# Two moves at the seam of a spectral kernel: constants and first weights made a stage earlier, and two engines reading a set of sums side by side

## The chip, the cores and the metric

The kernel runs on one core of a Trainium2 chip. The metric is device time in microseconds (us) of one launch, all transfers between HBM and the core's memory (SBUF) included. Five engines share the work: PE (matrix multiplies into PSUM[...]), ACT and DVE (elementwise work; both can read PSUM), POOL (elementwise work in SBUF) and SP, which here only issues DMA transfers. Each engine runs its own instructions in order and waits on semaphores for the others.

## The reference

Two layers on an image batch x of shape (16, 16, 256, 256), float32. Layer 0 adds a 3x3 circular convolution, done through FFTs, of the group-normalised input. Layer 1 adds a Laplace-pole layer. Cut to what matters:

```python
x = x + conv(_gn(x), L0_conv_weight)
v = _gn(x)
alpha = fft2(v)
A  = 1 / (omega1[:, None, None, None] - pole1[None])
Bm = 1 / (omega2[:, None, None, None] - pole2[None])
S = einsum('ikpq,oikp,xikq->oxik', residue, A, Bm)
residue1 = einsum('biox,oxik->bkox', alpha, S)
x1 = ifft2(residue1).real
x2 = transient(alpha, A, Bm, residue, exp(pole1 * ty), exp(pole2 * tx))
out = x + x1 + x2
```

For each frequency (o, x), S is a 16 x 16 complex matrix that mixes the input channels into the output channels. It is a sum over the poles q of a factor that depends on o and a factor Bm that depends on x.

## The kernel before

The kernel has four stages, one after the other. Stage 1 (0 to about 590 us) is the convolution and the statistics for the norms; it also makes tables, among them cD, the part of S that depends on o, and leaves v in HBM (vD). Stage 2, the forward transform (about 590 to 1213 us), takes v to frequencies: 64 units, each one channel i and four images b0. Stage 3, the mixing (to about 1895 us), applies S. Stage 4 transforms back and adds the transient part.

**Forward stage.** For each unit, `fold` (L734 to L755) adds and subtracts mirrored halves of the image: DVE makes most of it, POOL the second part of vq (L750 and L751 called with POOL). `lines` (L758) multiplies on PE (L762, L770), and ACT scales the result into t (L778). `columns` (L785) multiplies again on PE (L790 for the projections psd, L805 for ps_x); ACT copies the odd half to q (L818), and DVE combines both into spec (L822 to L825). `first_slots` (L828) corrects single frequencies on DVE (L833) and POOL (L834). After the last four images of a channel, `project` multiplies psd by coefficients on DVE (L850) and POOL adds to proj (L851), and spec is written to HBM (aD, L891, 4 MB). The loop works one unit ahead: in iteration u it folds unit u + 1, runs lines of unit u and columns of unit u - 1. PSUM: three banks for ps_y, four for ps_x, one for psd.

**Mixing stage.** The 256 x-frequencies are taken as 128 partitions of work in 32 groups g, each with four quarters n. For each group, `weights(g)` makes Bm times a mask: DVE computes the complex reciprocals in four steps (L957 to L973) and a last multiply spreads them over the mask, on POOL (L983); for group 0 three ACT copies (L979) and one POOL operation (L980) do this. For group 32, the frequency 128, POOL does it. `sums(n, w)` multiplies the weights with ct, the SBUF copy of cD (L1012): 16 small products into two PSUM banks, called odd = 0 and 1. `spread` (L1023) takes each bank into sg, the mixing matrices: ACT writes one half with a sign (L1027), DVE a partition-shuffled half (L1028). Both read the same bank, so they are ordered one after the other.

`first_sums` (L1030) prepares group 0. Frequencies 0 and 128 share a slot there, so it runs eight sets of sums (four with w, four with w128); for each bank it calls spread twice, for the main part (128 frequencies) and for two single columns (`other`). Between sets it runs the steps of weights(1). It also clears `pair` (abd for quarters 0 and 1, L1035) and abd2, abd3 (L1055) on POOL, loads group 0 of aD (L1076, L1081), and sums proj into accs (L1038). Then the loop over g and n runs, all in the order written (a manual schedule): sums for group g + 1; two spreads; four `mix` products (L1094) into four PSUM banks, each copied to yt by ACT or DVE (L1207); loads of group g + 1 (`load`, L1068) and the store of yt to HBM (`store`, L1106, four DMAs). yt has two buffers. All these DMAs are issued on SP, in the order of the code:

```python
if n == 1 and g < 31:
    load(g + 1, n)
store(g, n, yt)
if n > 1 and g < 31:
    load(g + 1, n)
```

`pair` serves quarters 0 and 1, so load(g + 1, 1) waits for quarter 1's products. Beside this, `make_exps` (L1135) makes tables of exponentials for stage 4, mostly on POOL, with ACT's table loads (L1172, L1175).

Each stage has its memory pools on a stack; stage 3's are opened after stage 2's have been closed, and a tile that comes to lie on memory of stage 2 waits for the last use there. Within stage 2 and 3 each engine keeps the written order, apart from the seam, where instructions of stage 3 may stand ahead of the last ones of stage 2.

Of the kernel before, what the change touches and what calls it, by code (L numbers as in the profile page):

```python
# [9 lines left out]
FP = mybir.dt.float32  # L10
# [6 lines left out]
B = 16  # L17
C = 16
# [6 lines left out]
def conv_then_laplace_kernel(ctx: ExitStack, tc: tile.TileContext, a: dict, out: bass.AP):  # L25
# [829 lines left out]
    units = [(i, b0) for i in range(C) for b0 in range(0, B, 4)]  # L855

    loaded = {u: load_v(*units[u], nc.sync if u else nc.gpsimd) for u in range(3)}
    vq = fold(*units[0], loaded.pop(0))
    nc.vector.memset(sgn[:, 0:1], -1.0)
    nc.vector.memset(sgn[:, 1:2], 1.0)  # L860
    rest = v_stats(B - 4, B, lambda: pa.tile([P, 512], FP, name="ps_y", tag="ps_y"))
    last = None
    for u in range(len(units) + 1):
        at = units[u] if u < len(units) else None
        if at is not None:
            now = vq
            t = lp.tile([P, 2, 4, 3, P], FP, name="t", tag="t")
            if u + 1 < len(units):
                vq = fold(*units[u + 1], loaded.pop(u + 1))
# [12 lines left out]
        if at is not None:  # L882
            for j in range(2, 4):
                lines(*at, now, t, j)
                if u < 2:
                    next(rest, None)
        if last is not None:
            first_slots(b0, spec, *done)
            if b0 == B - 4:
                project(i, psd)  # L890
                (nc.sync if i + 1 < C else nc.scalar).dma_start(  # L891
                    out=aD[:, 2 * i : 2 * i + 2].rearrange("p r n -> p (r n)"),
                    in_=spec.rearrange("p r f b -> p (r f b)"),
                )
        last = (*at, t) if at is not None else None
    p1.close()
    ptab.close()


    p2 = ExitStack()  # L900

    yp = pool(p2, "yt", 2)
    g0 = pool(p2, "sg0")
    a0 = pool(p2, "abd0")
    wp = pool(p2, "w", 2)
    ep = pool(p2, "exps")
    kp = pool(p2, "m_const")
    up = pool(p2, "uv")
    a1 = pool(p2, "abd2")
    zp = pool(p2, "between")  # L910
    tp = pool(p2, "ct")
    a2 = pool(p2, "abd3")
    g1 = pool(p2, "sg1")
    pg = pool(p2, "p_s", 4, space=PSUM)
    pm = pool(p2, "p_mix", 4, space=PSUM)

    def new_sg(g):
        return (g0, g1)[g % 2].tile([P, N, 2 * C], FP, name="sg", tag="sg")

    pair = a0.tile([P, 4, 4, 2, 16, B], FP, name="abd01", tag="abd01")
# [11 lines left out]
    omega(omg, omg, rd[:, 1:2])  # L934
# [8 lines left out]
    nc.vector.tensor_scalar(pims, p2k[:, :, 1], sset, None, ALU.mult)  # L943
    nc.vector.tensor_tensor(prU[:, 0], p2k[:, :, 0], p2k[:, :, 0], ALU.mult)

    nc.vector.tensor_scalar(prU[:, 1], p2k[:, :, 0], m0, -1.0, ALU.mult, ALU.mult)
    nc.vector.tensor_scalar(prU[:, 2], p2k[:, :, 0], m1, -1.0, ALU.mult, ALU.mult)

    def weights(g):

        shape = [P, 32, 4]
        u = up.tile([P, 4, 32, 4], FP, name="u", tag="u")
        w, den, e, f = (u[:, j] for j in range(4))
        pr2, pre, pim = (prU[:, j].unsqueeze(2).to_broadcast(shape) for j in range(3))
        nc.vector.tensor_tensor(  # L957
            w,
            omg[:, g].unsqueeze(1).to_broadcast(shape),
            pims.unsqueeze(2).to_broadcast(shape),  # L960
            ALU.subtract,
        )
        nc.vector.tensor_tensor(den, w, w, ALU.mult)
        nc.vector.tensor_tensor(den, den, pr2, ALU.add)
        yield
        nc.vector.reciprocal(den, den)

        nc.vector.scalar_tensor_tensor(e, w, m1, pre, ALU.mult, ALU.add)
        nc.vector.scalar_tensor_tensor(f, w, nm0, pim, ALU.mult, ALU.add)
        yield  # L970
        v = up.tile([P, 32, 2, 4], FP, name="v", tag="v")
        nc.vector.tensor_tensor(v[:, :, 0], e, den, ALU.mult)
        nc.vector.tensor_tensor(v[:, :, 1], f, den, ALU.mult)  # L973
        wt = wp.tile([P, 4, 8, 32], FP, name="w", tag="w")
        v2 = v.rearrange("p a r s -> p a (r s)")
        w4 = wt.rearrange("p a k (i m) -> p (a k) i m", i=4)
        if g == 0:
            for i in range(3):
                nc.scalar.activation(w4[:, :, i], v2, AF.Copy, scale=m4[:, i : i + 1])  # L979
            nc.gpsimd.tensor_scalar(w4[:, :, 3], v2, m4[:, 3:4], None, ALU.mult)  # L980
            return wt
        full = [P, 32, 4, 8]
        nc.gpsimd.tensor_tensor(  # L983
            w4,
            v2.unsqueeze(2).to_broadcast(full),
            m4.unsqueeze(1).unsqueeze(3).to_broadcast(full),
            ALU.mult,
        )
        return wt

    def next_step(steps, w):
# [31 lines left out]
    def spread(to, n, odd, src):  # L1023


        k = 4 * n + 2 * odd
        nc.scalar.activation(to[..., k : k + 2], src, AF.Copy, scale=nsgn)  # L1027
        nc.vector.stream_shuffle(to[..., C + k : C + k + 2], src, swap)  # L1028

    def first_sums():  # L1030
# [3 lines left out]
        wt, w128 = at_once(weights(0)), at_once(weights(32))  # L1034
        nc.gpsimd.memset(pair, 0.0)  # L1035
        load(0, 1)
# [4 lines left out]
        for h, w in enumerate((wt, w128)):  # L1041
            for n in range(4):
                fy = slice(P * h, P * h + P)
                ps = sums(n, w)
                for odd in range(2):
                    spread(sg[:, fy], n, odd, ps[odd][:, :, fy].rearrange("p q n -> p n q"))
                    spread(other[:, 1 - h], n, odd, ps[odd][:, :, P * (1 - h)])
# [20 lines left out]
    def load(g, jq):  # L1068
# [4 lines left out]
        for s in range(4):  # L1073
# [122 lines left out]
    for g in range(32):  # L1196
# [3 lines left out]
        for n in range(4):  # L1200
            evict = sums(n, w_now) if ahead is not None else []
            yt = yp.tile([P, 2, 4 * B, 16], FP, name="yt", tag="yt")
            for odd, ps in enumerate(evict):
                spread(ahead, n, odd, ps.rearrange("p q n -> p n q"))
# [3 lines left out]
            if n == 1 and g < 31:  # L1208
                load(g + 1, n)
            store(g, n, yt)  # L1210
            if n > 1 and g < 31:
                load(g + 1, n)
# [372 lines left out]
```

## Time and profile before

| what | us |
|---|---|
| median of 3 runs | 2682.2 (2677.55 to 2683.32) |
| the profiled execution | 2672.83 |
| its span, first to last instruction | 2670.8 |
| PE busy | 2492.1 (93%) |
| DVE busy | 1991.5 (75%) |
| ACT busy | 1448.6 (54%) |
| POOL busy | 1310.0 (49%) |
| last forward matmul (L805) starts | 1211.57, for 1.95 |
| first matmul of sums (L1012) starts | 1224.58 |
| first mixing matmul (L1094) starts | 1252.27 |

The profile gives, for one execution, when each instruction ran and what it waited for. "POOL L851 TENSOR_TENSOR proj<-proj,pr ... x2 [0.99 <-DVE pr L850]" reads: POOL ran two additions of line 851 that write proj; before them it sat idle 0.99 us, until DVE's pr of line 850 was there. SPq, ACTq are the DMA-issuing queues of SP and ACT. A chain of 60% PE means that most of the chain of work that ended last is PE's.

### The profile page before, as it was taken

What the parts mean: (1) busy time and instruction counts of PE and PEld (TensorE: products, weight loads), DVE (VectorE), ACT (ScalarE), POOL (GpSimd) and SP (SyncE); (2) the same over time, 40 slices, a digit from 0 to 9 for tenths busy, and PEclk for the clock granted to TensorE, in tenths of its full rate; (3) what the DMA queues carried; (4) which work ended last, traced back from release to release, by engine and by line L of the source; (5) the groups of instructions that cost most, each with busy time, mean ns of one, the idle gap of its engine ahead of it and who ended that gap; (6) DMA issues with size and microseconds to landing.
All of it is one profiled execution on the core that took longest, in us unless ns stands there. A gap on an engine that the chain in (4) does not pass through costs nothing.

```text
span 2670.8 us, 84449 instructions
## 1 busy us (share of the span) xinstructions
PE 2492.1 (93%) x35314; PEld 1877.6 (70%) x35314; DVE 1991.5 (75%) x3805; ACT 1448.6 (54%) x2726; POOL 1310.0 (49%) x1182
## 2 busy tenths in 40 slices
PE   5998899889999999997999999999699999999998
PEld 2444454457777777774877778887588888888887
DVE  7767689748888888887788778787366776666666
ACT  2565566566666666664666656666244444444443
POOL 1333368342333333333566755766546565555653
PEclk9999999989999999997999999999899999999999
DMA  7888978865556655664777777777889999898985
GB/s 273 276 278 275 282 251 301 270 207 174 212 198 237 237 207 196 245 229 154 216 230 224 226 223 232 213 223 228 233 279 287 288 287 290 278 291 283 293 279 178
DMA packets 476828, 653.17 MB, mean 245 GB/s; under 512 B 51063, under 2 KB 426999, under 8 KB 466593
## 3 DMA queue, kind: packets, MB, share of 16 engines
q1 hardware_dynamic: 475376, 640.58, 74.9%
q8 instruction: 278, 4.55, 0.7%
q0 software_dynamic: 928, 3.02, 0.4%
q10 hardware_dynamic: 144, 4.19, 0.4%
q14 instruction: 102, 0.83, 0.1%
HBM read 368.15 MB, written 280.36 MB: 243 GB/s over the span
## 4 chain that ended last, share of the span: by engine, by line
PE 60%; DMA 15%; DVE 13%; SPq 4%; issue 3%; POOL 3%; ACT 2%; DVEq 0%; ACTq 0%; POOLq 0%
PE ps_conv L294 14%; PE ps_y L762 9%; PE ps_mix L1094 8%; PE ps_y L770 8%; DMA yk<-yD 6%; PE ps_x L805 4%; DMA out_y<-ol 4%; DMA yD<-yt 4%; PE ps_p L1337 3%; DVE r L1370 3%; PE ps_f L1361 3%; PE ps_f L1362 3%; PE ps_s L1012 2%; DVE ol L1373 2%; DVE sg L1028 2%
## 5 line engine op out<-in xcount | busy, mean ns | idle before, releaser
L1094 PE MATMUL ps_mix<-abd,sg 128*64 128x128 f32 x8192 | 482.2, 276 | 35.5 <-ACT yt L1207 25.1
L1094 PEld LDWEIGHTS ps_mix<-abd,sg 128*64 128x64 f32 x8192 | 448.2, 138 | 92.7 <-ACT yt L1207 49.9
L1301 POOL TENSOR_TENSOR u<-yk 128x512 f32<-128x512 f32 (+1 forms) x268 | 346.3, 1323 | 311.6 <-PE ps_p L1337 203.9
L294 PE MATMUL ps_conv<-xt,wc 32*32 32x512 f32 x12288 | 449.1, 615 | 47.7 <-issue 41.6
L294 PEld LDWEIGHTS ps_conv<-xt,wc 32*32 32x32 f32 x12288 | 251.1, 104 | 234.0 <-issue 153.5
L778 ACT ACTIVATE t<-ps_y,vmr 128x384 f32<-128x384 f32 x512 | 297.5, 581 | 162.7 <-PE ps_y L770 162.6
L1028 DVE STREAM_SHUFFLE sg<-ps_s 128x512 f32<-128x512 f32 (+1 forms) x264 | 326.0, 1325 | 0.0
L762 PE MATMUL ps_y<-tabE,vq 128*128 128x256 f32 x1024 | 313.5, 388 | 13.2 <-DVE vq L751 11.7
L264 POOL TENSOR_TENSOR vt<-vt 128x1024 f32<-128x1024 f32 x64 | 151.7, 2371 | 324.8 <-DVE vsum L261 256.0
L770 PE MATMUL ps_y<-tabO,vq 128*128 128x256 f32 x1024 | 306.0, 381 | 0.0
L1337 PEld LDWEIGHTS ps_p<-inv,u 128*128 128x128 f32 x2048 | 266.2, 193 | 50.4 <-issue 25.5
L1361 PE MATMUL ps_f<-pt,inv 128*128 128x256 f32 x1008 | 301.3, 381 | 0.0
L1362 PE MATMUL ps_f<-hs,ey 128*128 128x256 f32 x1008 | 300.4, 380 | 0.0
L1365 DVE TENSOR_TENSOR r<-ps_f,q 128x256 f32<-128x256 f32 x256 | 107.3, 419 | 254.6 <-ACT q L1364 254.6
L1337 PE MATMUL ps_p<-inv,u 128*128 128x128 f32 x2048 | 279.5, 280 | 13.2 <-POOL u L1305 13.1
L1207 ACT COPY yt<-ps_mix 128x512 f32<-128x512 f32 x352 | 191.2, 593 | 152.0 <-DMA yD<-yt 100.5
L309 ACT ACTIVATE vt<-ps_conv,xq 128x512 f32<-128x512 f32 x256 | 162.2, 684 | 181.4 <-PE ps_conv L294 181.4
L1364 ACT COPY q<-ps_f 128x256 f32<-128x256 f32 x256 | 95.4, 373 | 290.6 <-PE ps_f L1362 284.7
L762 PEld LDWEIGHTS ps_y<-tabE,vq 128*128 128x128 f32 x1024 | 189.7, 191 | 89.7 <-ACT q L818 50.3
L750 POOL TENSOR_TENSOR vq<-vf 128x512 f32<-128x512 f32 x64 | 81.4, 1272 | 293.2 <-DVE vf L754 270.6
L1339 ACT COPY pt<-ps_p 128x512 f32<-128x512 f32 x256 | 150.2, 587 | 137.1 <-PE ps_p L1337 132.7
L770 PEld LDWEIGHTS ps_y<-tabO,vq 128*128 128x128 f32 x1024 | 195.6, 191 | 27.0
(239 smaller groups left out, 4067.5 us busy)
## 6 DMA issues: line engine op xcount, KB each, us to landing
yD<-yt SPq DMA_DIRECT2D x512, 128.0 KB, 3.4
vl<-vD SPq DMA_DIRECT2D x256, 256.0 KB, 3.8
out_y<-ol SPq DMA_DIRECT2D x128, 512.0 KB, 10.0
s<-vD SPq DMA_DIRECT2D x252, 256.0 KB, 5.9
aD<-spec SPq DMA_DIRECT2D x15, 4096.0 KB, 13.1
yk<-yD SPq DMA_DIRECT2D x60, 1024.0 KB, 8.4
xt<-in_x SPq DMA_DIRECT2D x64, 645.0 KB, 6.2
xt<-in_x SPq DMA_DIRECT2D x64, 516.0 KB, 6.9
```

The source lines that it names most:

```text
L294: nc.tensor.matmul(acc[r][32 * c : 32 * c + 32], lhsT=ready[b][0][rows, phase, tap], rhs=halves[b][u // 2][rows, q : q + 5 : 4, 2 - tap : ...
L309: nc.scalar.activation(vt[:, r % 2], acc[r], AF.Identity, bias=ready[b][1])
L762: nc.tensor.matmul(ps[:, 0:N], lhsT=vf[:, xo, 0, j], rhs=tabE[:, 0 : i + 2 : i + 1], start=True, stop=False, skip_group_check=True,)
L770: nc.tensor.matmul(ps[:, P : P + N], lhsT=vf[:, xo, 1, j], rhs=tabO[:, i : C + 1 : C - i], start=False, stop=True, skip_group_check=True,)
L778: nc.scalar.activation(t[:, xo, j].rearrange("p l n -> p (l n)"), ps[:, 0:384], AF.Copy, scale=vmr[:, 0, b0 + j, i : i + 1],)
L1028: nc.vector.stream_shuffle(to[..., C + k : C + k + 2], src, swap)
L1094: nc.tensor.matmul(ps[64 * t : 64 * t + 64, j], lhsT=sg[:, f : f + 2].rearrange("p f m -> p (f m)"), rhs=abd[jq][:, :, 2 * t + cc, 2 * jj ...
L1207: (nc.vector.tensor_copy if m >= (2 if late else 3) else nc.scalar.copy)(o, src)
L1301: nc.gpsimd.tensor_tensor(u[:, :, j].rearrange("p b (c n) -> p c b n", c=8), in0, in1, o)
L1337: nc.tensor.matmul(ps[:, at], lhsT=u[:, n], rhs=tab, start=True, stop=True)
L1361: nc.tensor.matmul(ps[:, e], lhsT=tab, rhs=pt[:, e], start=True, stop=False)
L1362: nc.tensor.matmul(ps[:, e], lhsT=ey[:, e], rhs=hs, start=False, stop=True)
```

## The change

1. The pools for the mixing's constants (`m_const`) and weights (`uv`) are opened before the forward loop, on the other side of the memory. The three constant loads, `weights` and the constant operations move with them. `first_constants` is called in iteration 60; the first three steps of weights(0) run in iterations 61, 62 and 63. The masks of group 0 are now four ACT copies, and POOL's one operation goes.
2. `spread` takes both banks of a set: ACT reads bank 0 while DVE reads bank 1, and then they swap.
3. The clearing of `pair` stands ahead of the weights in `first_sums`.
4. In the loop, load(g + 1, 1) is split: rows 0 and 1 ahead of the store of quarter 1, rows 2 and 3 behind it.

```diff
@@ before the forward loop @@
     units = [(i, b0) for i in range(C) for b0 in range(0, B, 4)]
+    p2 = ExitStack()
+    kp = pool(p2, "m_const", side="right")
+    up = pool(p2, "uv", side="right")
+
+    p2k = kp.tile([P, 32, 2], FP, name="p2k", tag="p2k")
+    nc.sync.dma_start(out=p2k, in_=a["pole2_k"])
+    omg = kp.tile([P, 33, 4], FP, name="kgrp", tag="kgrp")
+    nc.sync.dma_start(out=omg, in_=a["kgrp"])
+    mcol = kp.tile([P, 11], FP, name="mcol", tag="mcol")
+    nc.sync.dma_start(out=mcol, in_=a["mcol"])
...
+    def first_constants():
+        omega(omg, omg, rd[:, 1:2])
+        nc.vector.tensor_scalar(pims, p2k[:, :, 1], sset, None, ALU.mult)
+        nc.vector.tensor_tensor(prU[:, 0], p2k[:, :, 0], p2k[:, :, 0], ALU.mult)
+
+        nc.vector.tensor_scalar(prU[:, 1], p2k[:, :, 0], m0, -1.0, ALU.mult, ALU.mult)
+        nc.vector.tensor_scalar(prU[:, 2], p2k[:, :, 0], m1, -1.0, ALU.mult, ALU.mult)
+
+    def weights(g):
...
+        nc.vector.tensor_tensor(v[:, :, 0], e, den, ALU.mult)
+        nc.vector.tensor_tensor(v[:, :, 1], f, den, ALU.mult)
+        if g == 0:
+            yield
+        wt = wp.tile([P, 4, 8, 32], FP, name="w", tag="w")
...
+        if g == 0:
+            for i in range(4):
+                nc.scalar.activation(w4[:, :, i], v2, AF.Copy, scale=m4[:, i : i + 1])
+            return wt
...
-    last = None
+    last, first_weights = None, weights(0)
     for u in range(len(units) + 1):
...
+        if u == len(units) - 4:
+            first_constants()
+        if len(units) - 4 < u < len(units):
+            next(first_weights)
         if last is not None:
             first_slots(b0, spec, *done)
...
-    def spread(to, n, odd, src):
-
-
-        k = 4 * n + 2 * odd
-        nc.scalar.activation(to[..., k : k + 2], src, AF.Copy, scale=nsgn)
-        nc.vector.stream_shuffle(to[..., C + k : C + k + 2], src, swap)
+    def spread(n, *pairs):
+
+
+        for odd in range(2):
+            for to, src in pairs:
+                k = 4 * n + 2 * odd
+                nc.scalar.activation(to[..., k : k + 2], src[odd], AF.Copy, scale=nsgn)
+            for to, src in pairs:
+                k = 4 * n + 2 * (1 - odd)
+                nc.vector.stream_shuffle(to[..., C + k : C + k + 2], src[1 - odd], swap)
...
-        wt, w128 = at_once(weights(0)), at_once(weights(32))
         nc.gpsimd.memset(pair, 0.0)
+        wt, w128 = at_once(first_weights), at_once(weights(32))
         load(0, 1)
...
-                for odd in range(2):
-                    spread(sg[:, fy], n, odd, ps[odd][:, :, fy].rearrange("p q n -> p n q"))
-                    spread(other[:, 1 - h], n, odd, ps[odd][:, :, P * (1 - h)])
+                spread(
+                    n,
+                    (sg[:, fy], [z[:, :, fy].rearrange("p q n -> p n q") for z in ps]),
+                    (other[:, 1 - h], [z[:, :, P * (1 - h)] for z in ps]),
+                )
...
-    def load(g, jq):
+    def load(g, jq, rows=range(4)):
...
-        for s in range(4):
+        for s in rows:
...
-            for odd, ps in enumerate(evict):
-                spread(ahead, n, odd, ps.rearrange("p q n -> p n q"))
+            if evict:
+                spread(n, (ahead, [z.rearrange("p q n -> p n q") for z in evict]))
...
             if n == 1 and g < 31:
-                load(g + 1, n)
+                load(g + 1, n, (0, 1))
             store(g, n, yt)
-            if n > 1 and g < 31:
-                load(g + 1, n)
+            if g < 31:
+                load(g + 1, n, (2, 3) if n == 1 else range(4))
```

More of the change, by code (lines that the diff above doesn't have):

```diff
@@ L855, in conv_then_laplace_kernel @@
     units = [(i, b0) for i in range(C) for b0 in range(0, B, 4)]
+    p2 = ExitStack()
[7 more added lines that the diff above has]
+    nc.sync.dma_start(out=mcol, in_=a["mcol"])
+    m4, sset, fixrow = mcol[:, 0:4], mcol[:, 4:5], mcol[:, 5:6]
@@ new lines, in conv_then_laplace_kernel @@
+    nsgn, first = mcol[:, 7:8], mcol[:, 8:9]
+    osgn, nosgn = mcol[:, 9:10], mcol[:, 10:11]
+    m0, m1, nm0 = cols[:, 0:1], cols[:, 1:2], cols[:, 9:10]
+    prU = kp.tile([P, 4, 32], FP, name="prU", tag="prU")
+    pims = kp.tile([P, 32], FP, name="pims", tag="pims")
+    def first_constants():
[4 more added lines that the diff above has]
+        nc.vector.tensor_scalar(prU[:, 2], p2k[:, :, 0], m1, -1.0, ALU.mult, ALU.mult)
@@ new lines, in weights @@
+    def weights(g):
+        shape = [P, 32, 4]
+        u = up.tile([P, 4, 32, 4], FP, name="u", tag="u")
+        w, den, e, f = (u[:, j] for j in range(4))
+        pr2, pre, pim = (prU[:, j].unsqueeze(2).to_broadcast(shape) for j in range(3))
+        nc.vector.tensor_tensor(
+            w,
+            omg[:, g].unsqueeze(1).to_broadcast(shape),
+            pims.unsqueeze(2).to_broadcast(shape),
+            ALU.subtract,
+        )
+        nc.vector.tensor_tensor(den, w, w, ALU.mult)
+        nc.vector.tensor_tensor(den, den, pr2, ALU.add)
+        yield
+        nc.vector.reciprocal(den, den)
+        nc.vector.scalar_tensor_tensor(e, w, m1, pre, ALU.mult, ALU.add)
+        nc.vector.scalar_tensor_tensor(f, w, nm0, pim, ALU.mult, ALU.add)
+        yield
+        v = up.tile([P, 32, 2, 4], FP, name="v", tag="v")
+        nc.vector.tensor_tensor(v[:, :, 0], e, den, ALU.mult)
+        nc.vector.tensor_tensor(v[:, :, 1], f, den, ALU.mult)
+        if g == 0:
+            yield
+        wt = wp.tile([P, 4, 8, 32], FP, name="w", tag="w")
+        v2 = v.rearrange("p a r s -> p a (r s)")
+        w4 = wt.rearrange("p a k (i m) -> p (a k) i m", i=4)
+        if g == 0:
+            for i in range(4):
+                nc.scalar.activation(w4[:, :, i], v2, AF.Copy, scale=m4[:, i : i + 1])
+            return wt
+        full = [P, 32, 4, 8]
+        nc.gpsimd.tensor_tensor(
+            w4,
+            v2.unsqueeze(2).to_broadcast(full),
+            m4.unsqueeze(1).unsqueeze(3).to_broadcast(full),
+            ALU.mult,
+        )
+        return wt
@@ L897, in conv_then_laplace_kernel @@
     ptab.close()
-    p2 = ExitStack()
     yp = pool(p2, "yt", 2)
@@ L906, in conv_then_laplace_kernel @@
     ep = pool(p2, "exps")
-    kp = pool(p2, "m_const")
-    up = pool(p2, "uv")
     a1 = pool(p2, "abd2")
@@ L929, in conv_then_laplace_kernel @@
     nc.sync.dma_start(out=ct, in_=cD)
-    p2k = kp.tile([P, 32, 2], FP, name="p2k", tag="p2k")
-    nc.sync.dma_start(out=p2k, in_=a["pole2_k"])
-    omg = kp.tile([P, 33, 4], FP, name="kgrp", tag="kgrp")
-    nc.sync.dma_start(out=omg, in_=a["kgrp"])
-    omega(omg, omg, rd[:, 1:2])
-    mcol = kp.tile([P, 11], FP, name="mcol", tag="mcol")
-    nc.sync.dma_start(out=mcol, in_=a["mcol"])
-    m4, sset, fixrow = mcol[:, 0:4], mcol[:, 4:5], mcol[:, 5:6]
-    nsgn, first = mcol[:, 7:8], mcol[:, 8:9]
@@ L939, in conv_then_laplace_kernel @@
-    osgn, nosgn = mcol[:, 9:10], mcol[:, 10:11]
-    m0, m1, nm0 = cols[:, 0:1], cols[:, 1:2], cols[:, 9:10]
-    prU = kp.tile([P, 4, 32], FP, name="prU", tag="prU")
-    pims = kp.tile([P, 32], FP, name="pims", tag="pims")
[L943 to L989, printed above, removed]
@@ L1044, in first_sums @@
                 ps = sums(n, w)
-                for odd in range(2):
-                    spread(sg[:, fy], n, odd, ps[odd][:, :, fy].rearrange("p q n -> p n q"))
-                    spread(other[:, 1 - h], n, odd, ps[odd][:, :, P * (1 - h)])
+                spread(
+                    n,
+                    (sg[:, fy], [z[:, :, fy].rearrange("p q n -> p n q") for z in ps]),
+                    (other[:, 1 - h], [z[:, :, P * (1 - h)] for z in ps]),
+                )
                 if 4 * h + n in (3, 4, 5):
```

## The prediction

> **What bounds the kernel now.** I read busy time by stretch first, cut where the engines' timelines change their lines. Columns: stretch, its length, then busy time (and instructions) of PE, PE's weight loads, DVE, ACT, POOL; granted clock; DMA share; GB/s.
>
> ```profile
> 590.00:1211.60 621.60, 615.37 (x4088) 443.76 (x4088) 522.40 (x1191) 371.56 (x639) 220.16 (x282) 0.99 0.61 216
> 1211.60:1252.30 40.70, 24.26 (x316) 10.35 (x313) 30.15 (x109) 12.74 (x37) 18.80 (x10) 0.66 0.33 130
> 1252.30:1891.00 638.70, 602.18 (x12152) 508.51 (x12160) 497.00 (x904) 405.55 (x680) 384.35 (x295) 0.99 0.77 224
> ```
>
> The forward stage is PE's (99% busy). The mixing loop is nearly PE's: 36.5 us without a matmul in 638.7. Between them lies a seam of 40.7 us, where PE's few matmuls are stretched by waits. The change touches the seam and the loop.
>
> Second, the seam's timelines. DVE, with rows left out between:
>
> ```profile
> 1217.92 0.98 DVE L75 TENSOR_SCALAR kgrp<-kgrp,rd 128x132 f32<-128x132 f32 x1
> 1218.82 1.25 DVE L943 TENSOR_SCALAR pims<-p2k,mcol 128x32 f32<-128x32 f32 x1
> ...
> 1222.85 0.29 DVE L973 TENSOR_TENSOR v<-u 128x128 f32<-128x128 f32 x1
> ...
> 1227.14 0.75 DVE L1028 STREAM_SHUFFLE sg<-ps_s 128x256 f32<-128x256 f32 x1
> ...
> 1251.69 0.19 DVE L1052 TENSOR_TENSOR other<-other,sg 128x32 f32<-128x32 f32 x1
> ```
>
> POOL and ACT there:
>
> ```profile
> 1217.55 2.48 POOL L851 TENSOR_TENSOR proj<-proj,pr 128x512 f32<-128x512 f32 x2 [0.99 <-DVE pr L850]
> 1223.40 0.94 POOL L980 TENSOR_SCALAR w<-v,mcol 128x256 f32<-128x256 f32 x1 [3.37 <-DVE v L973]
> 1226.34 2.18 POOL L983 TENSOR_TENSOR w<-v,mcol 128x1024 f32<-128x1024 f32 x1 [2.00 <-DVE v L973]
> 1228.46 6.92 POOL L1035 MEMSET abd<- 128x8192 f32 x1
> ```
>
> ```profile
> 1216.89 0.34 ACTq L891 DMA_DIRECT2D aD<-spec  x1
> ...
> 1227.92 0.26 ACT L1027 ACTIVATE other<-ps_s,mcol 128x2 f32<-128x2 f32 x1 [0.82 <-DVE sg L1028]
> ```
>
> The reader is to see: PE's last forward matmul ends at 1213.5, yet its first sum starts at 1224.58, behind constants, weights and POOL's copy of them. Then ACT and DVE take turns: ACT waits for DVE 0.82 us, DVE for ACT. Eight sets of sums take 1227.14 to 1251.65.
>
> Third, the loop: its waits (who waited for whom: total us, times, longest), the SP queue, and one stall.
>
> ```profile
> ACT yt L1207 <- DMA yD<-yt: 100.5, 51, 8.5
> DVE sg L1028 <- ACT sg L1027: 90.0, 68, 3.7
> PE ps_mix L1094 <- ACT yt L1207: 25.1, 22, 5.8
> ```
>
> ```profile
> 1282.18 3.17 SPq L1076 DMA_DIRECT2D abd<-aD  x4
> 1285.46 5.41 SPq L1108 DMA_DIRECT2D yD<-yt  x8
> ```
>
> ```profile
> 1291.92 3.71 PE L1094 MATMUL ps_mix<-abd,sg 128*64 128x128 f32 x64 [1.84 <-ACT yt L1207]
> ```
>
> Four loads (3.2 us) stand in SP's queue before the stores of quarter n=1. Those land about 1291.2, so ACT can first write that yt buffer again, for n=3, at 1291.29. PE wants the bank, for the next group's n=0, and stalls 1.84. I counted PE's gaps over 0.15 us by place in the group: n=0 18.5 us in 19 gaps; n=1 6.2 in 7; n=3 4.1 in 8, and 5.8 at the loop's very end.
>
> **What the skill says.** The Trainium skill, "PSUM — Partial Sum Buffer", section "PSUM bank collisions raise a hardware error", says that two engines must not touch one bank and quadrant at once, ACT and DVE reads included. So turn-taking is kept within a bank; the trace agrees (the 0.82 us waits). "SBUF — State Buffer", section "SBUF: two separate sides": DVE and GpSimd share a port pair under an exclusive lock; a DVE op with two SBUF inputs is held only against a GpSimd op that reads SBUF. The trace fits: L75 and L943 took 0.98 and 1.25 us, each ending with one of POOL's proj additions, while L1052, with two SBUF inputs, took 0.19 during a memset.
>
> **The change part by part.**
>
> *Forward stage.* Five constant operations enter unit 60: 0.18 to 0.23 us each by the prU rows, starts 0.10 to 0.15 apart, so 0.8 us. They push the fold on DVE, then POOL's half (L750, L751), which ended 1190.94. PE needed it from about 1191.85, so 0.9 of slack covers them. First weights in unit 61 take 0.95 us (three operations); PE's slack at the next fold is 2.2, of which 1.8 is used. Unit 62's step falls into a 6.15 us DVE gap. I take +0.5, bounds 0 and +2 (a lock wait on top). The three constant DMAs move from behind ct to SP's queue before a pair of vD stores at about 524; their 1.2 us of issue fit a 3.6 us gap there: nothing.
>
> *Start of the seam.* In the order listing of the changed program, DVE makes v(0) and all of weights(32) before the last spec operations; ACT makes the four copies of w before the last q copies. DVE has 3.44 us idle there (1209.95 to 1213.38) and needs 0.4 + 2.9; ACT has 1.84 idle and needs 4 x 0.41 = 1.7. They just fit. PE's first sums can then start near 1213.5. But POOL's order becomes: memset (6.92), the last two corrections of spec, w(32), proj. The memset starts when POOL is free, 1209.8 to 1210.4, and ends about 1217.2. Corrections to 1217.6 (before 1216.57), w(32) 2.0 to 1219.6, proj 2.48 to 1222.1. accs (L1038 before) waits for proj, 0.7, and the shuffles queue behind accs: first shuffle 1222.8 instead of 1227.14. Gain 4.3.
>
> *Eight sets.* The same 32 main and small pairs, but in each half ACT reads one bank while DVE reads the other, then they swap. A half costs DVE about 0.7 (0.75 + 0.16 with the overlap of consecutive starts), so a set about 1.4; before, two turns of 1.43 made 2.9. 8 x 1.4 + 2.5 for the three steps of weights(1) = 13.7, and the row fixes 0.8: 1237.3. PE must still run its projection matmuls (3.5) and the loop's first sums (1.0) after the last set, which puts the first mixing matmul at about 1238.6 against 1252.3. The loads it needs: the last aD write, issued 0.7 later, lands 13.1 on, 1230.8; SP issues four loads in 2.5, last landing 4.3 on: 1237.6. This floor is a microsecond under. Seam: -13.7; bounds -10 (set costs 1.8) and -15 (the load floor). If the memset did hold DVE's weights, spec and aD would be 6.5 late and the seam would give only about 7.
>
> *The loop's load split.* Two of four loads go behind the stores of n=1: stores start up to 1.25 us earlier. Each n=0 gap shrinks by at most that: 18.5 becomes 2.5, so at most 16. The two later loads end about 9 us after n=1's mixing; they are needed 10.4 after. Because SP issues as many DMAs as before, and a removed stall exposes the next wait (POOL's w, ACT's table loads), I count 8.
>
> *The loop's evictions.* DVE no longer waits for ACT's first copy (90 us of waiting), but DVE idles later instead, for PE's fourth tile, so most of it is no gain; where ACT is late behind a table load, DVE's first shuffle is free, which should take part of the n=1 gaps: 3 us. Against this, ACT's second copy now waits for DVE's first shuffle (1.31 us against 0.57 spacing): yt copies behind it on ACT, and so the stores, start 0.7 later, more when DVE is held by a reciprocal. ACT is 63% busy there, and PE hides it while ACT's third copy ends within the 4.67 us of a quarter; 2.04 + 3 x 0.55 = 3.7 does. Cost 1, bounds 0 and 30. Loop: -10, bounds -22 (the n=0 and n=1 gaps gone) and +15.
>
> Sum: 0.5 - 13.7 - 10 = -23. The profiled execution took 2672.83 (span 2670.8), so 2649.8; the runs' median is 2682.2, 0.35% higher, so 2659 there.
>
> **Rivals.**
> 1. Only the seam gives; the loop is unchanged because SP's queue stays as full (28 issues of about 0.5 us in 18.7): 2682 - 13 = 2669. For it: stores in runs of eight with SP seldom idle. Against: the gaps sit at one place in the group.
> 2. POOL's early memset decides: spec, aD and proj late, the seam gives 5 to 7, the loop little: 2674. Against: L1052's 0.19.
> 3. More: all gaps at n=0 and n=1 go: 2682 - 36 = 2646. Against: SP.
> 4. Slower: ACT is held by DVE. It decides from the point where DVE reaches the first shuffle over 1 us after PE's sums are ready: then 1 + 1.31 + 0.7 + 1.65 fills a quarter. At 0.25 us in each of 124 sets it costs 31 us, against the seam's 13.7 and 2 from the load split: 2682 + 15 = 2697. For it: DVE is the busiest of the three (78%), and its 128x128 operations stretch from 0.28 to 1.3 us beside POOL's exponentials. Against: the wait list shows ACT late more often than DVE.
>
> **How the numbers follow.** Forecast 0.50, seam alone 0.21, memset 0.09, more 0.08, slower 0.12. About 0.2% (5 us) can be told from no change here. Forecast, seam and more are faster; of memset's 0.09 0.04 is faster, 0.05 the same; slower keeps 0.11 and gives 0.01 to no change: 0.83, 0.06, 0.11. The range runs from 2644 (rival 3 with the runs' spread of 3) to 2677 (memset, same spread).
>
> **What would show it.** Right: sums at about 1213.5, first shuffle near 1223, first mixing matmul 1237 to 1240; no turn of ACT and DVE on the small copies; n=0 gaps mostly gone. Wrong: forward PE gaps over 2 us at lines L762; new waits of ACT's sg copy on DVE's shuffle that end in PE gaps; abd loads arriving after PE asks; DVE's weights stretched beside the memset. A loop longer than 640 us would make the sign wrong.

## The result, and the profile after

The changed kernel took 2663.39 us (median of 15 runs, 2654.82 to 2673.96) against 2679.33 for the kernel before on the same chips (15 runs, 2672.73 to 2686.58). The ratio is 0.9946, with a 95% interval of 0.9932 to 0.9959: 14.5 us faster by the ratio, give or take 3.6. The forecast was 23 us faster.

The one profiled execution of each kernel must not be set against the other as a whole. The one before took 2672.83 and is near the fast end of its kind. The one after took 2673.96 and is the slowest of its 15. So the stages are compared, cut at the same events in each trace. The table has the execution before and the one after; the last column is the spread over the other profiled executions of this study.

| stretch, from event to event | before | after | how much it moves where the program has the same text |
|---|---|---|---|
| start to first ps_y (stage 1) | 594.3 | 598.2 | 587.2 to 600.5 |
| forward: to the start of the last L805 group | 617.2 | 617.6 | 617.0 to 618.0 |
| seam: to the first mixing matmul | 40.7 | 38.5 | within 0.25, one execution 1.5 off |
| mixing: to the end of the last one | 638.6 | 640.2 | 638.6 to 650.7 with the old loop |
| the rest | 780.0 | 777.4 | 769.8 to 777.8 |

The forward stage and the seam can be read from one trace to a fraction of a microsecond. Stage 1 and the last stage move by 8 to 13 us from one execution to the next, without any change to their instructions. What the change does to the mixing loop is therefore read from medians, after taking the seam out.

Busy time by stretch, of the kernel after, with the columns of the same view before (length; PE, weight loads, DVE, ACT, POOL; clock; DMA share; GB/s):

```profile
598.25:1215.88 617.63, 615.73 (x4084) 443.92 (x4084) 523.68 (x1203) 371.54 (x641) 221.38 (x283) 0.99 0.59 208
1215.88:1254.36 38.48, 16.40 (x315) 9.01 (x312) 21.75 (x95) 11.72 (x37) 13.82 (x8) 0.73 0.64 247
1254.36:1894.53 640.17, 603.96 (x12147) 514.56 (x12146) 503.35 (x902) 407.06 (x680) 388.79 (x298) 0.98 0.76 224
```

The seam lost 8.4 us of DVE's work (30.15 to 21.75), 5 of POOL's and 8 of PE's, yet it is only 2.2 us shorter. Its DMA share went up, from 0.33 to 0.64: a transfer has come into it. The timeline of the seam after, all engines, in order of time:

```profile
1214.42 6.93 POOL L1043 MEMSET abd<- 128x8192 f32 x1 [0.39 <-POOL spec L834]
...
1215.88 1.95 PE L805 MATMUL ps_x<-t,fold 64*64 64x512 f32 x16
...
1216.87 0.29 DVE L903 TENSOR_TENSOR v<-u 128x128 f32<-128x128 f32 x1
1217.08 0.29 DVE L904 TENSOR_TENSOR v<-u 128x128 f32<-128x128 f32 x1
...
1217.94 0.33 SPq L995 DMA_DIRECT2D ct<-cD  x1
...
1221.69 0.34 ACTq L961 DMA_DIRECT2D aD<-spec  x1
...
1225.97 0.69 DVE L1047 TENSOR_TENSOR accs<-proj 128x512 f32<-128x512 f32 x1 [3.64 <-POOL proj L851]
...
1236.24 6.72 PE L1017 MATMUL ps_s<-ct,w 64*32 64x256 f32 x128 [18.41 <-DMA ct<-cD]
...
1238.33 0.01 DVE L1037 LOAD_MASK_SELECT sg<-ps_s  x1 [11.67 <-PE ps_s L1017]
1238.33 0.73 DVE L1037 STREAM_SHUFFLE sg<-ps_s 128x256 f32<-128x256 f32 x1
```

The reader is to see: the load of ct, 4 MB, is issued at 1217.94, just after PE's last product of the forward stage has ended (1215.88 + 1.95 = 1217.83). It lands 18.3 us later; the last write of aD, also 4 MB, starts 3.75 us after it. PE stands 18.41 us for it, and DVE, ready since accs ended at 1226.66, stands 11.67 us. Everything that the change made early waits at that one door. Weights, accs and memset were all done by 1226.7. In the kernel before, the same load was issued 17 us ahead of PE's last product (1211.57), and the first sums waited for POOL's copy of the weights:

```profile
1194.45 0.33 SPq L929 DMA_DIRECT2D ct<-cD  x1
...
1224.58 3.67 PE L1012 MATMUL ps_s<-ct,w 64*32 64x256 f32 x64 [11.06 <-POOL w L980]
```

Why the load is late can't be seen in the diff; it is in the addresses of the built program. Each stage's pools stand on a stack. Before, m_const and uv (4.72 KB per partition together) lay below ct, which began at 143.75 KB. The change takes them to the other end of the memory, so ct slides down to 139.03 KB. The second buffer of t, the copy from which PE reads the forward stage's last products, ends at 141.09 KB. An overlap of 2.06 KB out of ct's 32 is enough: the whole load waits for PE's last reading of t.

The waits of the kernel after (who waited for whom: total us, times, longest):

```profile
ACT sg L1034 <- DVE sg L1037: 117.9, 100, 3.4
...
ACT yt L1218 <- DMA yD<-yt: 38.7, 25, 8.8
...
DVE sg L1037 <- ACT sg L1034: 29.3, 22, 2.5
...
PE ps_mix L1105 <- ACT yt L1218: 14.5, 11, 5.8
...
PE ps_mix L1105 <- DMA yD<-yt: 8.6, 9, 2.7
...
PE ps_mix L1105 <- DMA abd<-aD: 5.8, 3, 3.2
```

Against the lines shown of before: ACT's waiting for its yt buffer fell from 100.5 to 38.7 us, and PE's for ACT's copies from 25.1 to 14.5. DVE's wait for ACT at the evictions fell from 90.0 to 29.3, but the opposite wait, ACT for DVE, is now 117.9. And PE now stands 14.4 us for transfers, laid to stores (yD) and to loads (abd), where before none of its waits in the loop was laid to either. By the kernel's text all of this must be for loads: a mixing product reads abd and sg, and no store. Loads and stores take turns on the same eight semaphores in the trace, so the profile can name a store where PE waited for a load.

### The profile page after: what moved, and what is told of

Read it like the earlier page. It is cut to its first block, busy times and chain, and to the rows that moved or that the text cites. A ratio compares the mean times of both kernels' runs of the same rounds, so it can differ in the third digit from the quotient of the medians.

```text
span 2672.0 us, 84459 instructions
## 1 busy us (share of the span) xinstructions
PE 2486.5 (93%) x35314; PEld 1882.8 (70%) x35314; DVE 1994.7 (75%) x3805; ACT 1448.0 (54%) x2727; POOL 1311.7 (49%) x1181
## 4 chain that ended last, share of the span: by engine, by line
PE 68%; DMA 12%; DVE 10%; SPq 5%; issue 3%; ACT 2%; POOL 0%; DVEq 0%; ACTq 0%; POOLq 0%
PE ps_conv L294 16%; PE ps_mix L1105 11%; PE ps_y L762 9%; PE ps_y L770 8%; PE ps_p L1348 5%; PE ps_x L805 4%; PE ps_f L1372 4%; PE ps_f L1373 4%; DMA yk<-yD 4%; DMA yD<-yt 3%; PE ps_s L1017 3%; DVE r L1381 2%; SPq L1119 2%; DMA out_y<-ol 2%; PE psd L790 1%
## 5 line engine op out<-in xcount | busy, mean ns | idle before, releaser
L1105 PE MATMUL ps_mix<-abd,sg 128*64 128x128 f32 x8192 | 484.5, 277 | 36.2 <-ACT yt L1218 14.5
L1105 PEld LDWEIGHTS ps_mix<-abd,sg 128*64 128x64 f32 x8192 | 454.4, 139 | 89.3 <-ACT yt L1218 47.8
L762 PE MATMUL ps_y<-tabE,vq 128*128 128x256 f32 x1024 | 313.5, 388 | 13.2 <-DVE vq L751 11.7
L1348 PEld LDWEIGHTS ps_p<-inv,u 128*128 128x128 f32 x2048 | 266.0, 193 | 50.2 <-issue 25.1
L1348 PE MATMUL ps_p<-inv,u 128*128 128x128 f32 x2048 | 279.4, 280 | 13.2 <-POOL u L1316 13.1
L1034 ACT ACTIVATE sg<-ps_s,mcol 128x512 f32<-128x512 f32 (+1 forms) x264 | 179.5, 689 | 201.9 <-DVE sg L1037 117.9
## 6 DMA issues: line engine op xcount, KB each, us to landing
aD<-spec SPq DMA_DIRECT2D x15, 4096.0 KB, 13.2
```

What stands on the lines that cost most here:

```text
L762: nc.tensor.matmul(ps[:, 0:N], lhsT=vf[:, xo, 0, j], rhs=tabE[:, 0 : i + 2 : i + 1], start=True, stop=False, skip_group_check=True,)
L1034: nc.scalar.activation(to[..., k : k + 2], src[odd], AF.Copy, scale=nsgn)
L1105: nc.tensor.matmul(ps[64 * t : 64 * t + 64, j], lhsT=sg[:, f : f + 2].rearrange("p f m -> p (f m)"), rhs=abd[jq][:, :, 2 * t + cc, 2 * jj ...
L1348: nc.tensor.matmul(ps[:, at], lhsT=u[:, n], rhs=tab, start=True, stop=True)
```

## The experiments

Each kernel was timed beside the kernel before, on the same chip. Two theories stand at the start. The place of ct: the seam's expected gain is all there, hidden behind a load that the new memory layout made late. The rival: the seam's order itself (the memset first, POOL's w and proj behind it) costs what it saves.

**1. ct back in its place.** One pool is opened later. t comes to lie at 109 to 133 KB, clear of ct; what lies under the start of ct is now vf, whose readers are done earlier.

```diff
     sp = pool(p1, "fold_y", 3)
-    f1 = pool(p1, "fold_1")
     fp = pool(p1, "fold_2", 2)
     lp = pool(p1, "lines", 2)
+    f1 = pool(p1, "fold_1")
```

> The changed kernel with one forward pool (fold_1) moved behind the pool of t, so that ct no longer lies on memory of t. Theory A (place): the sums of the seam wait for ct because its memory was t's until the last ps_x product. Then ct is loaded about 19 us sooner, lands before the sums want it, and the first sums start within 4 us of the last forward product instead of 20.4; first mixing product 24 to 28 us after the start of the last ps_x product instead of 38.5; time 2652 +- 4, ratio to before 0.990. Rival B (the shuffles are held by POOL's clearing, proj and accs anyway, and the 4 MB write of spec by the DMA engines): the seam gives at most 4 us more than the changed kernel, 2659 to 2663.

Measured: 2647.3 us, ratio 0.9884 (0.9865 to 0.9904). The stretch of its seam, columns as above, and then its timeline, all engines:

```profile
1204.72:1230.05 25.33, 16.38 (x315) 8.55 (x312) 23.42 (x95) 12.36 (x38) 14.59 (x8) 0.80 0.53 209
```

```profile
1193.10 0.33 SPq L995 DMA_DIRECT2D ct<-cD  x1
...
1203.57 6.93 POOL L1043 MEMSET abd<- 128x8192 f32 x1 [0.71 <-PE ps_y L770]
...
1209.02 2.54 PE L1017 MATMUL ps_s<-ct,w 64*32 64x256 f32 x64 [2.35 <-ACT w L912]
...
1210.77 2.53 POOL L851 TENSOR_TENSOR proj<-proj,pr 128x512 f32<-128x512 f32 x2
...
1210.84 0.34 ACTq L961 DMA_DIRECT2D aD<-spec  x1
1211.07 1.10 DVE L903 TENSOR_TENSOR v<-u 128x128 f32<-128x128 f32 x1
...
1212.10 1.34 DVE L904 TENSOR_TENSOR v<-u 128x128 f32<-128x128 f32 x1
...
1213.98 0.72 DVE L1037 STREAM_SHUFFLE sg<-ps_s 128x256 f32<-128x256 f32 x1
```

ct is issued at 1193.10, early again, 11.6 us ahead of the last forward products (1204.72). The sums start 4.3 us after those, where it was 20.4 in the kernel after, and the first mixing matmul comes 25.3 us after them instead of 38.5. The write of aD, alone on the DMA engines, is ready for the next load 11.7 us after its issue (the load goes out at 1222.59); in the kernel after it was 20.4. The memset is first in POOL's order here too, so the rival falls: nothing of the 13.2 us was the memset's.

The edit has a side effect. The order that the engines got at the seam differs from the kernel after: ACT makes the copies of w behind its last q copies (so the sums wait 2.35 us for them), and POOL adds to proj ahead of w of group 32, not behind it. accs, which waits for proj, was done 10.8 us after the last forward group's start in the kernel after, and the first shuffle came 9.3 after it here. So up to about 1.5 of the 13.2 us (an estimate from these two figures) may be due to this order and not to ct.

**2 to 4. The parts of the loop, with the seam mended.** Without the split of the load (all four rows ahead of the store), without the side-by-side evictions in the loop, and without both:

```diff
-                load(g + 1, n, (0, 1))
+                load(g + 1, n)
             store(g, n, yt)
-            if g < 31:
-                load(g + 1, n, (2, 3) if n == 1 else range(4))
+            if n > 1 and g < 31:
+                load(g + 1, n)
```

```diff
-            if evict:
-                spread(n, (ahead, [z.rearrange("p q n -> p n q") for z in evict]))
+            for odd, ps in enumerate(evict):
+                k, src = 4 * n + 2 * odd, ps.rearrange("p q n -> p n q")
+                nc.scalar.activation(ahead[..., k : k + 2], src, AF.Copy, scale=nsgn)
+                nc.vector.stream_shuffle(ahead[..., C + k : C + k + 2], src, swap)
```

The first diff is experiment 2, the second experiment 3, and both together experiment 4.

> As e1_ct_back, but the loop's load of quarter 1 is whole again, ahead of the store. Theory L1 (the loop's gain is the split's): the loop gives back 8 us, 2660. Theory L2 (the gain is the evictions', and late rows 2 and 3 eat the split's): within 2 us of e1_ct_back.

> As e1_ct_back, but the loop's evictions are in the old order (ACT then DVE on each bank); the seam keeps the new one. L1: within 2 us of e1_ct_back. L2: the loop gives back 8 us or so, 2660. If ACT is held by DVE (the slower rival of the prediction), this one is faster than e1_ct_back by 5 us or more.

> As e1_ct_back, with neither the split nor the new evictions in the loop: the seam alone. By the working of the prediction the seam is worth 13 to 14 us: 2666. If L1 and L2 are both partly right, it is slower than e1_ct_back by 10 us; if the loop gained nothing from either, it equals e1_ct_back.

Measured: 2657.27 us (0.992, 0.9896 to 0.9943), 2649.86 (0.9891, 0.9869 to 0.9913) and 2666.95 (0.995, 0.9931 to 0.9969). The waits of experiment 4, with the loop as before, and then of experiment 3, with the split alone:

```profile
ACT yt L1220 <- DMA yD<-yt: 113.9, 46, 9.5
...
PE ps_mix L1105 <- ACT yt L1220: 34.2, 26, 7.1
```

```profile
ACT yt L1220 <- DMA yD<-yt: 73.2, 55, 3.7
...
PE ps_mix L1105 <- DMA yD<-yt: 11.5, 9, 2.1
...
PE ps_mix L1105 <- ACT yt L1220: 7.7, 5, 5.6
...
PE ps_mix L1105 <- DMA abd<-aD: 5.7, 7, 2.2
```

In these two executions the split takes 26 us from PE's wait for ACT's copies (17 if the kernel before, with 25.1, is taken for the old loop), and 11.5 and 5.7 come back as waits laid to stores and to loads. One of the first kind, in experiment 3:

```profile
1267.88 1.26 SPq L1087 DMA_DIRECT2D abd<-aD  x2
...
1273.97 3.71 PE L1105 MATMUL ps_mix<-abd,sg 128*64 128x128 f32 x64 [2.09 <-DMA yD<-yt]
```

The last of these two rows is issued at 1268.44 and lands, by the trace's semaphore updates, at 1273.61; PE starts a group 0.36 us later. So it waited for a row that the split had put behind the store. By the medians the split gives 17.1 us without the loop's evictions (2666.95 to 2649.86, intervals apart) and 10.0 beside them (2657.27 to 2647.3, intervals that overlap a little). The evictions side by side give 9.7 us without it (2666.95 to 2657.27, intervals that overlap a little) and 2.6 with it (2649.86 to 2647.3), which is inside the noise. By these medians, and by experiments 8 and 9, the split carries more of the loop than the evictions do.

**5. The place of ct by itself, in the kernel before.** Only the order of the pools is changed, so that ct slides onto t there too.

```diff
     ep = pool(p2, "exps")
-    kp = pool(p2, "m_const")
-    up = pool(p2, "uv")
     a1 = pool(p2, "abd2")
     zp = pool(p2, "between")
     tp = pool(p2, "ct")
+    kp = pool(p2, "m_const")
+    up = pool(p2, "uv")
```

> The kernel before, with only the order of its pools changed: m_const and uv stand behind the pool of ct, so ct begins 4.72 KB lower in each partition and overlaps the second buffer of t, as it does in the changed kernel. No instruction is added, removed or reordered in the text. Theory (the place of ct decides when PE can start the sums): ct's load is issued only after the last ps_x product, near 1213.5 to 1217 instead of 1194.5, lands some 18 us later beside the aD write, and the first sums start near 1232 to 1236 instead of 1224.6: slower by 7 to 12 us, ratio 1.003 to 1.0045. Rival (ct's late load in the changed kernel is only the result of the new order of instructions at the seam): ct is issued near 1194 as before and the time stays within 3 us.

Measured: 2681.04 us, ratio 1.001 (0.9999 to 1.002), 3.7 us above the median beside it: the right sign at most, and a miss in size. Its timeline of the seam, all engines:

```profile
1199.17 0.35 SPq L931 DMA_DIRECT2D p2k<-in_pole_k  x1
...
1216.37 1.95 PE L805 MATMUL ps_x<-t,fold 64*64 64x512 f32 x16
...
1218.41 0.33 SPq L929 DMA_DIRECT2D ct<-cD  x1
...
1219.52 6.92 POOL L1035 MEMSET abd<- 128x8192 f32 x1
...
1226.79 0.34 ACTq L891 DMA_DIRECT2D aD<-spec  x1
...
1231.82 3.67 PE L1012 MATMUL ps_s<-ct,w 64*32 64x256 f32 x64 [13.50 <-DMA ct<-cD]
```

The mechanism is as expected: ct is issued 0.1 us after PE's last product (1218.32). The price is not. The load took 13.4 us, not 18; the write of aD went out 8.4 us after it instead of 3.75. And the edit had a second effect: the constants, freed from the memory that they had waited for, were loaded at 1199.17, before the forward stage's end, and the weights were ready. So the sums start 15.45 us after the start of the last products against 13.01 in the kernel before: 2.4 us, and the seam is 43.05 against 40.7. The sums start when the later of the two is there. Set against weights that come at 13.01, a ct that comes at 15.45 costs little; set against early ones it costs 12 to 13 (kernel after against experiment 1), and early is just what the change had made them.

**6. The seam's sets in turns again**, on top of experiment 1: in `spread`, if two pairs are given, ACT and DVE take one bank after the other as before.

```diff
+        if len(pairs) == 2:
+            for odd in range(2):
+                k = 4 * n + 2 * odd
+                for to, src in pairs:
+                    nc.scalar.activation(to[..., k : k + 2], src[odd], AF.Copy, scale=nsgn)
+                    nc.vector.stream_shuffle(to[..., C + k : C + k + 2], src[odd], swap)
+            return
```

> The changed kernel with ct in its old place (as in e1_ct_back), and the eight sets of the seam evicted in turns again, bank after bank; the loop keeps its side-by-side evictions. Theory (set cost decides): 8 sets times about 1.4 us, so the seam grows by 8 to 12 us and the time by as much, to about 2656 to 2659. Rival (the load of the first aD rows was the floor of the seam anyway, by at most a microsecond or so): the seam grows by no more than 3 us. The seam is read from the start of the last forward group of L805 to the first mixing matmul, 25.3 us in e1_ct_back.

Measured: 2658.56 us (0.993, 0.9905 to 0.9956). The stretch of its seam, columns as above:

```profile
1213.45:1247.78 34.33, 22.88 (x316) 9.97 (x313) 25.38 (x93) 13.02 (x38) 16.78 (x9) 0.70 0.39 154
```

34.3 us against 25.3: the side-by-side sets are worth 9.0 us of the seam, and the rest of what the change does there, above all the early constants and weights, 6.4 (40.7 - 34.3). The rival, by which the load of aD would hide all but 3 us of the first, falls.

**7. All four rows behind the store**, on top of experiment 1.

```diff
-            if n == 1 and g < 31:
-                load(g + 1, n, (0, 1))
             store(g, n, yt)
             if g < 31:
-                load(g + 1, n, (2, 3) if n == 1 else range(4))
+                load(g + 1, n)
```

> The changed kernel with ct in its old place, and all four loads for quarter 1 of the next group issued behind the store of quarter 1, where the change puts two ahead and two behind. Theory (the gain of the split is that the stores of quarter 1 start earlier, by 1.25 us with two loads moved and by 2.5 with four): as good as e1_ct_back or up to 5 us faster, 2642 to 2648. Rival (the loads have no time to spare: they are asked for about 10 us after the issue): PE waits for abd at quarter 1, slower than e1_ct_back by 5 us or more.

Measured: 2657.7 us (0.9918, 0.9894 to 0.9943), 10 us above experiment 1 (2647.3), 4 above its repeat below. So the theory, as good or better, isn't borne out; the rival's 5 us or more holds against the one set of runs and not against the other. Timeline of the first group, all engines:

```profile
1245.21 5.10 SPq L1119 DMA_DIRECT2D yD<-yt  x8
...
1250.40 2.46 SPq L1087 DMA_DIRECT2D abd<-aD  x4
...
1258.43 3.71 PE L1105 MATMUL ps_mix<-abd,sg 128*64 128x128 f32 x64 [2.29 <-DMA abd<-aD]
```

The loads are issued at 1250.40, behind eight stores, and PE, about to begin the next group, stands 2.29 us for the last. (The first quarter of the next group asks first, since one buffer serves quarters 0 and 1.) Over the loop this is, in its waits:

```profile
PE ps_mix L1105 <- DMA abd<-aD: 23.9, 16, 2.8
```

In experiment 1 the waits laid to loads and stores together are 17.7 us (5.6 and 12.1), in its repeat 24.8.

**8 and 9. The split alone, and the loop's side-by-side evictions alone, in the kernel before.** The edits are those of the change, each by itself.

> The kernel before with the split of the quarter-1 load alone: rows 0 and 1 ahead of the store, rows 2 and 3 behind it. Theory (the split carries the loop's gain by itself, and the side-by-side evictions only add where it is absent): faster by 10 to 17 us, 2662 to 2669, ratio 0.9936 to 0.996. Rival (the split gives only beside the other evictions or the new seam): 0 to 5 us.

> The kernel before with the loop's two evictions side by side alone; seam and loads as before. Theory (the two changes in the loop take time from the same stall, so each alone gives most of what it can): the seam stays 40.7 us and the loop gives what e2_no_split showed beyond its seam, about 7 us: 2669 to 2675, ratio 0.996 to 0.9985, and PE still waits 25 us or more for ACT's copies into yt. Rival (ACT is held by DVE's first shuffle, as the slower case of the prediction said): slower than before by 5 us or more.

Measured: 2666.46 us (0.9963, 0.9947 to 0.9978) and 2671.16 (0.9987, 0.9974 to 1.0). The split gives by itself about what it gives beside the rest; its theory holds, with a ratio at the edge of the expected range. The evictions alone are inside the expected times, but give only 3.5 us by the ratio, whose interval touches no change. Neither is slower: ACT being held by DVE (106.9 us over 89 waits in experiment 9) costs the loop nothing that can be measured. The waits of 8, then of 9:

```profile
PE ps_mix L1094 <- DMA yD<-yt: 12.5, 10, 2.6
...
PE ps_mix L1094 <- DMA abd<-aD: 7.2, 4, 2.2
...
PE ps_mix L1094 <- ACT yt L1207: 6.7, 5, 4.7
```

```profile
ACT sg L1206 <- DVE sg L1207: 106.9, 89, 2.6
...
PE ps_mix L1094 <- ACT yt L1210: 32.8, 20, 5.9
```

**10 to 12. Other splits, and experiment 1 once more.** Three rows ahead and one behind; one ahead and three behind; the kernel of experiment 1 again.

```diff
-                load(g + 1, n, (0, 1))
+                load(g + 1, n, (0, 1, 2))
-                load(g + 1, n, (2, 3) if n == 1 else range(4))
+                load(g + 1, n, (3,) if n == 1 else range(4))
```

This is experiment 10; in experiment 11 the rows are (0,) and (1, 2, 3).

> e1_ct_back with three rows of the load ahead of the store and one behind. With four ahead (e2_no_split) it was 2657.3, with two (e1_ct_back) 2647.3, with none (e7_load_behind) 2657.7. Theory (a balance of two waits: the stores' start, and the last rows' landing): between four and two, 2648 to 2654, with more of PE's waiting on ACT's yt copies and none on abd. Rival (the last row alone decides whether the store is early enough): as e1_ct_back within 2 us.

> e1_ct_back with one row of the load ahead of the store and three behind. Theory (a balance of two waits): between two and none, 2648 to 2655, with PE waiting for abd between the 5.6 us of e1_ct_back and the 23.9 of e7_load_behind. Rival (stores that start earlier still pay): 2644 or less.

> e1_ct_back once more, the same kernel in a second set of runs, because its place below three neighbours (one, three, or no row ahead: 2655 to 2658) rests on 6 runs. Theory (two rows ahead is the best of the splits): ratio 0.987 to 0.9905 again. Rival (its six runs were lucky): ratio 0.9915 or more, level with the neighbours.

Measured: 2655.06 us (0.9927, 0.9904 to 0.9949), 2655.64 (0.9923, 0.9901 to 0.9944), and 2653.9 (0.9904, 0.9878 to 0.9931) for the repeat. With three ahead, PE waits 20.2 us for ACT's copies, as its theory said (10.8 with two); no wait is laid to abd, but 7.7 us to stores, so the last row isn't quite out of the way. With one ahead the waits laid to loads and stores together are 18.1 us (4.4 and 13.7), hardly more than with two (17.7), where more was expected, so no wait explains why it is slower than two rows ahead. The three sets of runs with two rows ahead (experiments 1, 3 and 12: 0.9884, 0.9891, 0.9904) all lie below the four with other splits (0.9918 to 0.9927), but the intervals of 12 and of its neighbours overlap. That two rows is the best split is likely, and not settled.

Over both sets (12 runs) experiment 1 has a median of 2650.3 us, against 2679.8 for the kernel before beside it and 2663.39 for the kernel after. It beats both. Its text differs from the kernel after in one line, which moves a pool.

**What the loop gives in each.** The ratio times 2679.3 gives the difference in us; the seam's and the forward stage's parts are taken from the traces (each stretch against 40.7 and 617.2); what is left is the loop's, plus the noise of the medians (3 to 7 us).

| what the loop has | whole difference | seam and forward | left for the loop |
|---|---|---|---|
| split and evictions: after; experiments 1, 12, 6 | -14.5; -31.1, -25.7, -18.8 | -1.8; -15.0, -15.0, -6.5 | -12.7; -16.0, -10.7, -12.3 |
| split alone: 3, 8 | -29.2, -9.9 | -15.5, -0.2 | -13.7, -9.7 |
| evictions alone: 2, 9 | -21.4, -3.5 | -15.0, +0.8 | -6.4, -4.2 |
| evictions, other splits (0, 3, 1 rows ahead): 7, 10, 11 | -22.0, -19.6, -20.6 | -15.4, -14.6, -15.6 | -6.6, -4.9, -5.1 |
| neither: 4, 5 | -13.4, +2.7 | -15.5, +3.1 | +2.1, -0.4 |

In the row of experiment 12 the seam of experiment 1 is used. Its own profiled seam was 26.84, where PE's last set of sums took 2.08 us instead of 1.22. The profiled loops agree in the mean of each row: 644.5 us with neither (kernel before, 4 and 5; 638.6 to 650.7), 637.2 with the two-and-two split (six traces; 630.7 to 641.1), 642.1 with the evictions and no such split (five; 636.5 to 646.8).

**Where PE's gaps stand.** Counted as in the prediction (gaps over 0.15 us ahead of a mixing product, by the quarter n of the group), in us:

| loop | n=0 | n=1 | n=3 |
|---|---|---|---|
| as before: kernel before, 4, 5 | 18.5, 24.6, 23.9 | 6.2, 7.2, 6.3 | 9.9, 12.6, 10.7 |
| split two and two: after, 1, 3, 6, 8, 12 | 26.6, 26.3, 23.3, 22.0, 25.1, 25.9 | 0, 0, 1.6, 0, 0.6, 0 | 9.4, 10.6, 8.5, 6.5, 7.5, 12.4 |
| evictions, no such split: 2, 9, 7, 10, 11 | 26.8, 28.0, 30.8, 26.7, 24.5 | 0, 0, 0, 0, 0 | 12.9, 7.0, 8.9, 11.9, 10.9 |

The gaps at n=0, which the split was to remove, are all there. Only what ends them has changed: in the six traces with the two-and-two split, 113 of the 127 gaps at n=0 end within 0.6 us after the last row of the group's load has landed, whatever the wait is laid to. What has all but gone is the gaps at n=1, where PE had waited for DVE's copies into yt. Either move removes them by itself, which fits that the two gains don't add up.

## Why the prediction was right, and where it was wrong

The direction and the range were right, and the sum was 8 us too large. That hides two steps that failed, one at the seam and one in the loop. The prediction looked to the seam for most of the gain, and it came from the loop, the part with the wide bounds (-22 to +15). That the time fell into the range is in part luck.

*The start of the seam: failed.* The step is "PE's first sums can then start near 1213.5". It counted what stood between PE and the sums (constants, weights, POOL's copy of them), removed it, and took ct for given, which the trace before, with its load at 1194.45 and no wait for it, seemed to allow. The change moved 4.72 KB of pools out from below ct, and with them the address of ct and the tile that its load waits for. Sums were to start 1.9 us after the last forward group's start (1213.5 - 1211.57); they started 20.4 after it, and 4.3 with ct's place mended. Of the 13.7 us promised for the seam, 2.2 came. With the place mended it was 15.4.

*The rest of the seam: right in mechanism.* The first shuffle was put 11.2 us after the last forward group's start; it was 9.3 in experiment 1, where proj came ahead of w of group 32 on POOL. Eight sets with the steps of weights(1) were put at 13.7 us; from first shuffle to the fixes it took 15.1, in the kernel after and in experiment 1 alike. One set without such a step takes 1.43, as worked out (1.4). The fixes took 0.9 (0.8), and PE's projection ran beside the sets. The load of aD stayed just under, as worked out: in experiment 1 its last row, issued at 1224.51, lands 4.1 us later, at 1228.6, 1.5 us before the first mixing matmul. These errors nearly cancel (-15.4 for -13.7).

*The memset.* That it doesn't hold DVE's weights was taken from the Trainium skill, "SBUF — State Buffer", section "SBUF: two separate sides", which says that a DVE operation with two SBUF inputs is held only against a GpSimd operation that reads SBUF. The runs agree on both sides. In the kernel after, v of weights(32) (L903, L904) ran beside the memset in 0.29 us each. In experiment 1 the same two, each with two SBUF inputs, fell beside POOL's additions to proj and took 1.10 and 1.34. Rival 2, a late aD and late sums because of the memset, falls with it.

*The forward stage.* +0.5 promised, +0.4 measured, with constants of 0.19 to 0.28 us each; the stage scatters by 1.0 where its text is the same, so this is no more than agreement.

*The load split: about the right size, at the wrong place.* The term was 8 us; alone it measured 9.7 and 13.7 in the table, from which the noise hardly tells 8 apart. But the step "18.5 becomes 2.5" failed: with the split the gaps at n=0 are 22.0 to 26.6 us. It rested on the two later loads, which were to end about 9 us after n=1's mixing and be needed at 10.4. That 1.4 us to spare wasn't there: PE starts most groups just behind the landing of the last row. About 6 us of the gain is the gaps at n=1; where the rest comes from stays open. So this size is luck. The warning that "a removed stall exposes the next wait" came true, though with other names than POOL's w and ACT's table loads: the waits laid to loads and stores are 14 to 20 us over the loop in the kernel after and in experiments 1, 3 and 8.

*The loop's evictions: a small gain, as guessed.* The term was 2 us beside the split (3 gained, 1 lost); 2.6 was measured, inside the noise. Alone they give 4 to 6, and the gaps at n=1 are gone, of which the prediction gave them a part. DVE's wait moved to ACT, 117.9 us of it, and neither experiment 9 nor 3 shows a cost of it that can be measured; so rival 4 falls. That ACT has room (3.7 of 4.67 us in a quarter) was argued, and the runs don't speak against it.

*The sum.* -23 was +0.5, -13.7, -10. It was +0.4, -2.2, -12.7. Rival 1, by which only the seam gives, falls with experiment 8, and in the kernel after the loop gave most of the gain. Of the signs named for a wrong forecast, new waits of sg and of abd did appear in the loop, where the change as a whole saved more than they cost; and the loop was longer than 640 us (640.2), which was to make the sign wrong and didn't. With the old text it took 638.6 us in one execution and 644.1 and 650.7 in others, so one trace could not set that limit. Of the signs of being right, "n=0 gaps mostly gone" was not seen. The sign that mattered, a first sum that waits for ct, was not on the list.

## What to carry to other kernels

A pool that is moved moves every tile above it, and a load into one of those can come to wait for a tile that was nowhere near it in the code. So, for each load that a stage needs at its start, compare the addresses before and after, and name the last reader of what lies below it. And when a wait is removed, list everything that the waiting instruction reads, with the time at which each was there: the next latest is the bound, and if the change touches memory, it may itself have become later. Last, where a wait is laid to a transfer that the instruction doesn't read, look for one that it does read among those that share its semaphore.

## What the runs showed of the hardware

- Two transfers of 4 MB that overlap lengthen each other. ct took 13.3 us alone (kernel before) and 13.4 with the other started 8.4 us later (experiment 5), but 18.3 with one started 3.75 us later (kernel after). That other one, the write of aD, took 11.7 to the next load's issue in experiment 1, 14.9 in experiment 5 and 20.4 in the kernel after. There the two took 24.2 us together (1217.94 to 1242.14), about what they take one by one (13.3 + 11.7).
- Different stages scatter by very different amounts from execution to execution. The forward stage, whose PE is 99% busy, holds within 1.0 us in 617 over all profiled executions, while the stage before it moves by 13.
